# Conditioned ternary FFN on one Trainium2 core: the second block goes over from eight to seven products in its sixth chunk

## The chip, the cores and the metric

The kernel runs on one core of one Trainium2 chip. The core has five engines with a queue each: PE (TensorE, matmuls, with a separate weight load PEld), DVE (VectorE), ACT (ScalarE), POOL (GpSimd), and SP, which here only issues DMAs. Each queue runs its instructions in order; where one waits for another engine, all behind it wait too. The metric is the device time of one execution in microseconds, the median of three runs.

## The reference

`x` has the shape (128, 64, 512): 128 batch elements, 64 channels, 512 positions. Each batch element picks one of 200 weight matrices of 64 x 64, and its 64 x 512 slice is multiplied by it. The result goes through a feed-forward network whose two weight matrices are made ternary (each entry is -1, 0 or 1, times one scale alpha per matrix), and the output is rounded to 15 steps of one global scale and added to `x`:

```python
w = weights[conditions]
c = einsum('bct,bcd->bdt', x, w)                   # 128 x 64 x 512
h = gelu(c @ ternarize(W1).T + b1)                 # W1: 2048 x 512
y = h @ ternarize(W2).T + b2                       # W2: 512 x 2048
scale = max(abs(y)) / 7 + 1e-8
out = x + clip(round(y / scale), -7, 7) * scale
```

`ternarize` takes 0.05 of the largest absolute weight as its threshold; alpha is the mean absolute value of the weights above it. So alpha of W1 must be known before the first gelu, alpha of W2 before the first `y`.

## The kernel before

**Blocks and chunks.** The 8192 rows of the network (128 batch elements x 64) are worked in 16 blocks (`NB`) of 512 rows (`BLK`): eight batch elements each, as four pairs. The hidden width of 2048 is worked in 16 chunks (`NH`) of 128. For each block `n` and chunk `hc`, layer 1 multiplies the block's x (512 deep, four matmuls) by a chunk of W1 into PSUM, ACT takes the gelu, and layer 2 multiplies the result by the chunk's rows of W2 into four PSUM tiles `py0` to `py3`, which collect over all 16 chunks. Layer 2 of a chunk runs two steps after its layer 1 (`LAG = 2`).

**Two parts of everything.** Each operand is a sum of a high part in float32r and a low part in float16 (the remainder). Both are multiplied with the ternary weights. High products need the weights widened to float32r: POOL casts them (`widen1`, `widen2`, `widen7`). Low products take the narrow weights (float8, `w1t` and `w2t`) as they are. So layer 1 of a chunk is eight matmuls of 512 columns. ACT makes high parts (`split`, `up`), DVE makes low parts (`split`, `rest`, called by `low`).

**Eight products and seven.** From block 2 on, layer 1 is done for two chunks at a time by a scheme of Strassen's kind (`seven`): a two by two block product with seven half-size products in place of eight. It needs sums of the quarters of x (`condition7` makes them for the next block: `xb` the three quarters used as they are, `xt` the four sums, `xl` the low parts of all seven) and sums of the weights (`add_weights`, part 0 on POOL, part 1 on DVE, into `sums`). Its results are collected in the PSUM tiles `xy` and `z`, and put together by ACT copies and DVE adds into the buffers `ring`. Block 1 uses eight products in all its 16 steps (`eight`), and block 0 has a form of its own, while the weights are being made ternary.

**Order of the work.** The program's order is written out by hand: every engine call goes through `InOrder`, so the order of the Python calls is the order in each engine's queue. Pieces are placed behind matmuls by their step number: in `eight` by `hc`, in a pair by the calls `behind(0)` to `behind(6)` within `seven`.

**Around the change.** In the second half of block 0 (line 700 on) PE runs layer 2 of block 0. After its steps 5, 7, 9 and 11 one quarter of block 1's x is multiplied by its conditioned weights (`condition`, `mix`), ACT copies the high part, DVE subtracts for the low part, ACT counts the ternary entries of a quarter of W2 (`count2`) and casts that quarter to float8 (`kept(w2t, j, terns2)`), and DVE multiplies out the weights' sums (`sum2`). In block 1, step 1 finishes alpha of W2 (`alpha_2`) and the results of block 0 (`result`); step 2 takes the maxima of these results and stores them (`largest`, `keep`); steps 3 to 15 add up the weights for the seven products; steps 2 to 11 fetch, place and condition block 2's x; the last two steps widen the first weights for the seven products.

The pool `big` has 20 buffers of 8 KB a partition that are handed on from tile to tile; `ps_h` has two PSUM buffers, which layer 1's chunks take in turn, and later `xy`; `ps_c` has two, for the product of x with its weights, and later `z`.

Of the kernel before, what the change touches and what calls it, by code (L numbers as in the profile page):

```python
# [20 lines left out]
P = 128  # L21
# [18 lines left out]
def tile_cond_ternary_ffn(  # L40
# [26 lines left out]
    LAG = 2  # L67
    SEVEN = range(2, NB)
    HELD = NH // 2
# [3 lines left out]
    HALF = BLK // 2  # L73
    ADDED = [3, 4, 5, 6, 7, 12, 13, 14]

# [16 lines left out]
    def pair_of_pairs(h):  # L92
        return slice(h * PAIRS // 2, (h + 1) * PAIRS // 2)

    def load_x(n):

        xt = big.tile([P, PAIRS, T], F32, tag="big", name=f"xt_{n}")
# [92 lines left out]
    def parts(n):  # L190
# [268 lines left out]
    def layer2(n, hc, js=range(PAIRS), ks=(1, 0), ends=None):  # L459
        two = hidden[n, hc]  # L460
        w = wide2[n, hc], group2_of(hc) if n == 0 and hc < NH - LAG else w2t[:, hc]
# [238 lines left out]
    for hc in range(NH - LAG):  # L700
# [14 lines left out]
        if hc == 4:  # L715
            two_next = parts(1)
            w2t = big.tile([P, NH, T], F8, tag="big", name="w2t")
        if hc in (5, 7, 9, 11):
            j = (hc - 5) // 2
            condition(1, j, pair_of(x_next, j), two_next)  # L720
            count2(j)
            kept(w2t, j, terns2)
            if j == 0:
                signed2(3)
            if j == 1:
                for i in range(12, NH - 1):
                    low(0, i)
            for g in {9: [0, 1], 11: [2, 3]}.get(hc, []):
                sum2(g)
# [75 lines left out]
    def quarter_x(n, j):  # L805

        sp.dma_start(out=extra["x"][:, j % 2, :], in_=x_blk[n][:, j, :])

    def product(out, w, b, k, first=False, last=False):
        for c in range(2):  # L810
            pe.matmul(
                out=out,
                lhsT=w[k][:, c, :],
                rhs=b[k][:, c, :],
                start=(first and c == 0),
# [4 lines left out]
    def seven(n, k, behind, before, last):  # L820

        xb, xt, xl = cond[n]
        b11, b21, b22 = [(xb[:, i : i + 2], xl[:, i : i + 2]) for i in (0, 2, 4)]
        t1, t2, t3, t4 = [(xt[:, i : i + 2], xl[:, i + 6 : i + 8]) for i in (0, 2, 4, 6)]
        x, y = extra["xy"] if k % 2 == 0 else extra["xy"][::-1]
# [153 lines left out]
    def eight(s):  # L979

        n, hc = steps[s]
        if hc < NH - 1:
            widen1(n, hc + 1)
        else:
            widen7(0, 0)
        widen2(*steps[s + 1 - LAG])
        if hc == 0:
            extra["x"] = half.tile([P, 2, T], F32, tag="half", name="x_quarters")
            for j in range(2):
                quarter_x(n + 1, j)  # L990
# [17 lines left out]
        hidden[n, hc] = two  # L1008
        if hc == NH - 1:
            widen7(0, 1)  # L1010
        if 8 <= hc < 8 + PAIRS:
            j = hc - 8
            for part in condition7(n + 1, j, extra["x"][:, j % 2, :], two_next[-1]):
                part()
            if j + 2 < PAIRS:
                quarter_x(n + 1, j + 2)
            cond[n + 1] = two_next[-1]
        if hc == LAG:
            for j in range(PAIRS):
# [24 lines left out]
    def pair(n, k):  # L1044
# [10 lines left out]

        def behind(i):
            if i == 0 and n >= KNOWN:
                if n == KNOWN and k < 2:
# [186 lines left out]
```

## Time and profile before

| | |
|---|---|
| median of 3 runs | 963.0 us (962.86 to 963.06) |
| the profiled execution | 963.12 us |
| its span, from the first to the last instruction | 961.3 us |
| granted TensorE clock | 0.999 |
| PE busy | 949.9 us |
| POOL, DVE, ACT busy | 714.2, 710.6, 637.3 us |
| block 0, layer 2 begins | 51.49 us |
| block 1, layer 1 of its first chunk | 80.33 us |
| first pair with seven products (block 2) | 141.48 us |

Times in the traces are microseconds from the first instruction. A line of a timeline has start, duration, engine, kind, what it writes and reads with the shape, and in brackets how long the engine had been idle and which instruction released it. Buffer numbers are left out of names, so `x` stands for a tile of conditioned x, `ph` for a PSUM tile of layer 1, `py` for layer 2's. Consecutive matmuls overlap: a group's stated time is longer than the distance to the next one. As every call goes through one helper, all instructions show line 36 of the kernel; they are told apart by tile names.

### The profile page before, as it was taken

Reading aid. Unit: us, or ns where it says so; the run is one execution under the profiler, and the core shown is the slowest. Engines: PE = TensorE matmul, PEld = TensorE weight load, DVE = VectorE, ACT = ScalarE, POOL = GpSimd, SP = SyncE. Lnnn points to the kernel's source line nnn. Section 1 sums busy time; section 2 is a strip of 40 time slices with the busy share of each in tenths; the row PEclk is TensorE's granted clock in tenths of the full one; section 3 lists DMA queues with packets and bytes.
Section 4 is the critical chain, followed back from the end, with each engine's and each line's share of the span. In section 5 each row is a group of like instructions: output and inputs, shape, how many; then the busy total and the mean of one; then the engine's idle time right before and its main releaser. Section 6 shows DMA issues by size and latency. Waiting matters only on the chain.

```text
span 961.3 us, 17574 instructions
## 1 busy us (share of the span) xinstructions
PE 949.9 (99%) x6077; PEld 733.7 (76%) x6080; DVE 710.6 (74%) x1239; ACT 637.3 (66%) x1148; POOL 714.2 (74%) x1064
## 2 busy tenths in 40 slices
PE   8999999999999999999999999999999999999997
PEld 4666667888788787788778778788778878878784
DVE  7999766666676766666676676766667798888986
ACT  7995456656656566665666656666665777878784
POOL 5789867677686776767767686776768879788772
PEclk9999999999999999999999999999999999999999
DMA  9201011110111100111010111100131184575751
GB/s 357 105 23 47 14 33 49 32 62 15 35 48 35 60 24 25 52 41 49 25 70 14 35 50 33 59 26 24 49 121 60 49 304 170 180 248 169 276 203 62
DMA packets 33195, 80.11 MB, mean 83 GB/s; under 512 B 3792, under 2 KB 3792, under 8 KB 30160
## 3 DMA queue, kind: packets, MB, share of 16 engines
q1 hardware_dynamic: 31056, 76.86, 23.0%
q0 software_dynamic: 2048, 2.10, 0.7%
q8 instruction: 49, 0.80, 0.3%
q14 instruction: 42, 0.34, 0.1%
HBM read 46.44 MB, written 32.51 MB: 82 GB/s over the span
## 4 chain that ended last, share of the span: by engine, by line
PE 96%; DVE 2%; DMA 1%; ACT 0%; POOL 0%; issue 0%; SPq 0%; ACTq 0%
PE py L36 47%; PE xy L36 22%; PE z L36 16%; PE pc L36 6%; PE ph L36 6%; DVE top L36 1%; DMA nat<-in_L_ffn_W 1%; DVE xt L36 0%; DVE y_last L36 0%; ACT diag L36 0%; POOL wf L36 0%; PE number L36 0%; DVE terns L36 0%; DVE ymax L36 0%; DVE x L36 0%
## 5 line engine op out<-in xcount | busy, mean ns | idle before, releaser
L36 POOL CAST wf<-w2t 128x512 fp32r<-128x512 fp8e4 x240 | 228.8, 974 | 105.7 <-PE py L36 102.8
L36 PE MATMUL py<-wf,h 128*128 128x512 f32 x960 | 285.1, 418 | 0.0
L36 POOL CAST wf<-sums 128x256 fp32r<-128x256 fp8e4 (+1 forms) x336 | 182.6, 549 | 85.6 <-PE xy L36 81.9
L36 DVE SCALAR_TENSOR_TENSOR low_parts<-ring,h 128x512 f16<-128x512 f32 x228 | 203.0, 928 | 37.9 <-ACT h L36 37.7
L36 PE MATMUL py<-w2t,low_parts 128*128 128x512 fp8e4 x928 | 220.5, 379 | 0.0
L36 ACT ACTIVATE ring<-ring,b1t,alpha_up 128x512 f32<-128x512 f32 x216 | 175.2, 818 | 58.8 <-DVE ring L36 53.9
L36 DVE TENSOR_TENSOR ring<-xy,ring 128x256 f32<-128x256 f32 x216 | 119.8, 555 | 119.9 <-PE xy L36 118.4
L36 PEld LDWEIGHTS py<-wf,h 128*128 128x128 f32 x960 | 173.0, 189 | 39.1
L36 ACT COPY ring<-xy 128x256 f32<-128x256 f32 x216 | 80.6, 373 | 171.8 <-PE xy L36 171.2
L36 PEld LDWEIGHTS <-low_parts 128*128 128x128 f16 x928 | 90.4, 98 | 85.2 <-issue 0.3
L36 POOL CAST wf<-w1t 128x256 fp32r<-128x256 fp8e4 (+1 forms) x240 | 132.9, 570 | 2.8 <-POOL wf L36 0.4
L36 ACT ACTIVATE h<-ring 128x512 fp32r<-128x512 f32 x232 | 134.0, 627 | 0.6
L36 PE MATMUL xy<-xb,wf 128*128 128x256 f32 x448 | 98.8, 302 | 0.0
L36 PE MATMUL xy<-xt,wf 128*128 128x256 f32 x448 | 88.0, 277 | 0.0
L36 PE MATMUL xy<-xl,sums 128*128 128x256 f16 x448 | 87.9, 278 | 0.0
L36 PE MATMUL xy<-xl,w1t 128*128 128x256 f16 x448 | 86.8, 275 | 0.0
L36 PE MATMUL z<-xl,sums 128*128 128x256 f16 x448 | 85.5, 273 | 0.0
L36 PEld LDWEIGHTS xy<-xt,wf 128*128 128x128 f32 x448 | 76.3, 188 | 10.0
L36 PEld LDWEIGHTS xy<-xb,wf 128*128 128x128 f32 x448 | 75.9, 189 | 10.2
L36 PEld LDWEIGHTS <-sums 128*128 128x128 fp8e4 x896 | 69.2, 97 | 14.8
L36 POOL DMA_INDIRECT wg<-in_L_cond_weights,rows x64 | 64.2, 1003 | 18.3 <-issue 8.6
L36 PEld LDWEIGHTS <-w1t 128*128 128x128 fp8e4 x736 | 61.6, 98 | 18.1 <-issue 4.3
(139 smaller groups left out, 1410.0 us busy)
## 6 DMA issues: line engine op xcount, KB each, us to landing
xt<-in_x SPq DMA_DIRECT2D x36, 512.0 KB
y_dram<-y SPq DMA_DIRECT2D x15, 1024.0 KB
out<-xt SPq DMA_DIRECT2D x30, 512.0 KB
x_quarters<-in_x SPq DMA_DIRECT2D x56, 256.0 KB
nat<-in_L_ffn_W SPq DMA_DIRECT2D x6, 1024.0 KB
y_back<-y_dram SPq DMA_DIRECT2D x2, 1024.0 KB
nat<-in_L_ffn_W SPq DMA_DIRECT2D x3, 512.0 KB
wg<-in_L_cond_weights,rows POOLq DMA_INDIRECT x64, 2.5
```

Source lines behind the costliest of these rows:

```text
L36: return lambda *args, **kw: self._tc.keep_in_program_order(make(*args, **kw))
```

## The change

Block 1 uses eight products for its chunks 0 to 5 alone, and seven in five pairs for chunks 6 to 15 (`SWITCH = 3`: the first pair is number 3). For this:

- **The sums of block 1's x.** The quarters that the seven products need unsummed are read out of the existing `x0_1` and `x1_1` by strided views (`whole_parts`). For the sums, ACT keeps a float32 copy of the conditioned x: `condition(..., whole=True)` copies each PSUM tile once more, into the tile that x was loaded to. At the end of step 1 `sums_of_x` has DVE make the four sums in place (four instructions of 128x512) and ACT cast all of them to float32r (`xt_high`, 128x2048). In steps 3 and 4 `low_sums_of_x` makes their low parts (DVE, 128x1024 each).
- **W2 in float8.** The casts of quarters 2 and 3 (`kept(w2t, ...)`, ACT) move from block 0 into steps 0 and 1 of block 1. Layer 2 of block 0 takes narrow weights from `terns2` in all its chunks.
- **Sums of weights.** Numbers 3, 4 and 5 are made in steps 2 to 5, the rest within the pairs.
- **Maxima and store of block 0's results** move from step 2 to step 5. The first placement of block 2's conditioning weights moves from step 7 to step 5, the rest of block 2's conditioning into the pairs, as in other blocks. The gather of block 2's last quarter is issued in step 5 and once more in the first pair.

```diff
-    SEVEN = range(2, NB)
-    ADDED = [3, 4, 5, 6, 7, 12, 13, 14]
+    SWITCH = 3
...
+    def parts_of_1():
+        hi = big.tile([P, NT, BLK], F32R, tag="big", name="x0_1")
+        lows = big.tile([P, 2 * NT, BLK], F16, tag="big", name="x1_1")
+        high_sums = big.tile([P, PAIRS, T], F32R, tag="big", name="xt_high")
+        low_sums = lows[:, NT:, :].rearrange("p c t -> p (c t)")
+        return hi, lows[:, :NT, :], high_sums, low_sums.rearrange("p (j t) -> p j t", j=PAIRS)
...
-    def condition(n, j, xp, two):
+    def condition(n, j, xp, two, whole=False):
         pc = ps_c.tile([P, NT, P], F32, tag="pc", name=f"pc_{n}_{j}")
         mix(xp, j, pc)
         split(pc, *(t[:, :, j * P : (j + 1) * P] for t in two))
+        if whole:
+            act.copy(xp.rearrange("p (c t) -> p c t", c=NT), pc)
...
-            two_next = parts(1)
+            two_next = parts_of_1()
...
-            condition(1, j, pair_of(x_next, j), two_next)
+            condition(1, j, pair_of(x_next, j), two_next[:2], True)
             count2(j)
-            kept(w2t, j, terns2)
+            if j < 2:
+                kept(w2t, j, terns2)
...
+    def sums_of_x():
+        b11, b12, b21, b22 = (whole_sums(whole_x[1], r, h) for r in range(2) for h in range(2))
+        dve.tensor_tensor(b11, b12, b11, ALU.subtract)
+        dve.tensor_tensor(b12, b22, b12, ALU.subtract)
+        dve.tensor_tensor(b22, b22, b11, ALU.subtract)
+        dve.tensor_tensor(b21, b21, b22, ALU.subtract)
+        act.copy(cond[1][2], whole_x[1])
+
+    def low_sums_of_x(j):
+        js = pair_of_pairs(j)
+        dve.tensor_tensor(
+            cond[1][3][:, js], whole_x[1][:, js], cond[1][2][:, js], ALU.subtract
+        )
+
+    def whole_sums(t, r, h):
+        t = t.rearrange("p j (r c h d) -> p r c h j d", r=2, c=2, h=2)
+        return t[:, r, :, h]
+
+    def whole_parts(t, r, h):
+        t = t.rearrange("p (r c) (j h d) -> p r c h j d", r=2, h=2, d=C)
+        return t[:, r, :, h]
+
+    def operands(n):
+        if n == 1:
+            hi, lo, high_sums, low_sums = cond[n]
+            b = [(whole_parts(hi, *i), whole_parts(lo, *i)) for i in ((0, 0), (1, 0), (1, 1))]
+            t = [
+                (whole_sums(high_sums, *i), whole_sums(low_sums, *i))
+                for i in ((0, 0), (1, 1), (0, 1), (1, 0))
+            ]
...
     def eight(s):
         n, hc = steps[s]
-        if hc < NH - 1:
+        leaves = hc == 2 * SWITCH - 1
+        if not leaves:
             widen1(n, hc + 1)
         else:
-            widen7(0, 0)
+            widen7(SWITCH, 0)
         widen2(*steps[s + 1 - LAG])
...
+        if leaves:
+            place(n + 1, 0)
         if 2 <= hc < 2 + PAIRS:
             fetch(n + 1, hc - 2)
-        if 7 <= hc < 7 + PAIRS:
-            place(n + 1, hc - 7)
         for part in range(2):
-            if hc - part in ADDED:
-                add_weights(ADDED.index(hc - part), part)
-        if hc == NH - 2:
-            widen7(0, 2)
-            widen7(0, 3)
+            if 2 <= hc - part < 5:
+                add_weights(hc - part + 1, part)
+        if hc == 2 * SWITCH - 2:
+            widen7(SWITCH, 2)
+            widen7(SWITCH, 3)
+        if hc in (3, 4):
+            low_sums_of_x(hc - 3)
...
-        if hc == NH - 1:
-            widen7(0, 1)
-        if 8 <= hc < 8 + PAIRS:
...
+        if hc < 2:
+            kept(w2t, hc + 2, terns2)
+        if leaves:
+            widen7(SWITCH, 1)
-        if hc == LAG:
+        if hc == 2 * SWITCH - 1:
             for j in range(PAIRS):
                 largest(n - 1, j)
             keep(n - 1)
...
         low(n, hc)
+        if hc == 1:
+            sums_of_x()
...
         def behind(i):
+            if i == 0 and SWITCH < k + (n - 1) * NH // 2 <= NH // 2:
+                add_weights((k + 2) % (NH // 2), 1)
+            if i == 6 and n == 1:
+                add_weights((k + 3) % (NH // 2), 0)
...
-        if n in SEVEN:
-            if s == SEVEN[0] * NH:
+        if s >= NH + 2 * SWITCH:
+            if s == NH + 2 * SWITCH:
```

More of the change, by code (lines that the diff above doesn't have):

```diff
@@ L93, in pair_of_pairs @@
         return slice(h * PAIRS // 2, (h + 1) * PAIRS // 2)
+    whole_x = {}
     def load_x(n):
-        xt = big.tile([P, PAIRS, T], F32, tag="big", name=f"xt_{n}")
+        xt = whole_x[n] = big.tile([P, PAIRS, T], F32, tag="big", name=f"xt_{n}")
         for h in range(2):
@@ L460, in layer2 @@
         two = hidden[n, hc]
-        w = wide2[n, hc], group2_of(hc) if n == 0 and hc < NH - LAG else w2t[:, hc]
+        w = wide2[n, hc], group2_of(hc) if n == 0 else w2t[:, hc]
         begins, ends = ks[0], ks[-1] if ends is None else ends
@@ L807, in quarter_x @@
         sp.dma_start(out=extra["x"][:, j % 2, :], in_=x_blk[n][:, j, :])
+    def sums_of_x():
[24 more added lines that the diff above has]
+            ]
+        else:
+            xb, xt, xl = cond[n]
+            b = [(xb[:, i : i + 2], xl[:, i : i + 2]) for i in (0, 2, 4)]
+            t = [(xt[:, i : i + 2], xl[:, i + 6 : i + 8]) for i in (0, 2, 4, 6)]
+        return b + t
     def product(out, w, b, k, first=False, last=False):
@@ L813, in product @@
                 lhsT=w[k][:, c, :],
-                rhs=b[k][:, c, :],
+                rhs=b[k][:, c],
                 start=(first and c == 0),
@@ L820, in seven @@
     def seven(n, k, behind, before, last):
-        xb, xt, xl = cond[n]
-        b11, b21, b22 = [(xb[:, i : i + 2], xl[:, i : i + 2]) for i in (0, 2, 4)]
-        t1, t2, t3, t4 = [(xt[:, i : i + 2], xl[:, i + 6 : i + 8]) for i in (0, 2, 4, 6)]
+        b11, b21, b22, t1, t2, t3, t4 = operands(n)
         x, y = extra["xy"] if k % 2 == 0 else extra["xy"][::-1]
@@ L1008, in eight @@
         hidden[n, hc] = two
-        if hc == NH - 1:
-            widen7(0, 1)
-        if 8 <= hc < 8 + PAIRS:
[L1012 to L1017, printed above, removed]
-        if hc == LAG:
+        if hc < 2:
[3 more added lines that the diff above has]
+        if hc == 2 * SWITCH - 1:
             for j in range(PAIRS):
```

## The prediction

> **What bounds the kernel now.** I read four views of the profile in this order: the page's busy times and chain, the table of stretches across the end of the second block (block 1), the timelines of ScalarE (ACT), VectorE (DVE) and TensorE (PE) where block 0 hands over to block 1, and the groups of instructions by shape.
>
> ```profile
> PE 949.9 (99%) x6077; PEld 733.7 (76%) x6080; DVE 710.6 (74%) x1239; ACT 637.3 (66%) x1148; POOL 714.2 (74%) x1064
> ...
> PE 96%; DVE 2%; DMA 1%; ACT 0%; POOL 0%; issue 0%; SPq 0%; ACTq 0%
> ```
>
> PE is the bound: 949.9 of 961.3 us busy, 96% of the chain. Fewer products therefore show in the time, and so does every wait put in front of PE. The stretches below are two steps of eight products (127.14 and 134.32), three pairs of seven products without a product of x with its weights (148.28, 192.69, 199.50) and two pairs with one (161.89, 169.59).
>
> ```profile
> core 0: us, PE busy (x) PEld busy (x) DVE busy (x) ACT busy (x) POOL busy (x), PEclk, DMA share, GB/s
> 80.50:87.70 7.20, 7.20 (x35) 4.43 (x35) 6.96 (x11) 3.55 (x5) 7.17 (x5) 1.00 0.01 2
> ...
> 127.14:134.32 7.18, 7.18 (x34) 4.41 (x32) 5.15 (x11) 3.44 (x5) 6.12 (x8) 1.00 0.15 38
> 134.32:141.48 7.16, 7.16 (x34) 4.42 (x32) 4.58 (x7) 2.82 (x4) 5.85 (x9) 1.00 0.01 2
> ...
> 148.28:155.08 6.80, 6.80 (x45) 5.34 (x44) 6.47 (x11) 3.90 (x7) 5.28 (x9) 1.00 0.38 154
> ...
> 161.89:169.59 7.70, 7.70 (x54) 6.23 (x52) 4.57 (x12) 4.61 (x10) 6.61 (x12) 1.00 0.03 10
> 169.59:177.29 7.70, 7.70 (x54) 6.23 (x52) 5.26 (x13) 5.13 (x11) 5.67 (x10) 1.00 0.14 36
> ```
>
> PE has no idle time in any of them. But in the first stretch, where block 1 begins, DVE is busy 6.96 of 7.20 us and POOL (GpSimd) 7.17. That is where the change adds work, so I read it instruction by instruction. A line is start, duration, engine, what it writes and reads.
>
> ```profile
> 63.53 0.59 ACT L36 CAST x<-pc 128x512 fp32r<-128x512 f32 x1 [0.91 <-PE pc L36]
> 64.01 1.91 ACT L36 ACTIVATE masks<-terns 128x2048 bf16<-128x2048 bf16 x1
> 65.92 1.89 ACT L36 CAST w2t<-terns 128x2048 fp8e4<-128x2048 bf16 x1
> 68.00 0.59 ACT L36 CAST x<-pc 128x512 fp32r<-128x512 f32 x1 [0.20 <-PE pc L36]
> ...
> 72.48 0.59 ACT L36 CAST x<-pc 128x512 fp32r<-128x512 f32 x1 [0.20 <-PE pc L36]
> ```
>
> ```profile
> 65.15 0.68 DVE L36 TENSOR_TENSOR x<-pc,x 128x512 f16<-128x512 f32 x1
> ...
> 73.10 0.69 DVE L36 TENSOR_TENSOR x<-pc,x 128x512 f16<-128x512 f32 x1
> ...
> 79.20 0.68 DVE L36 TENSOR_TENSOR x<-pc,x 128x512 f16<-128x512 f32 x1
> ```
>
> ```profile
> 81.25 1.04 PE L36 MATMUL ph<-x,w1t 128*128 128x512 f16 x4
> ...
> 85.74 0.28 PE L36 MATMUL total<-sums,ones_f 128*128 128x8 f32 x2
> ...
> 94.87 1.08 PE L36 MATMUL ph<-x,wf 128*128 128x512 f32 x4
> ```
>
> ACT makes the high part of x for block 1 in four quarters (63.53, 68.00, 72.48, 76.95), DVE the low part (65.15, 69.87, 73.10, 79.20), and DVE does not idle once between 60 and 97 us. PE reads the last low part from 81.25, only 1.4 us after its end, and the sums for the second scale at 85.74, 0.7 us after DVE ends them (84.99).
>
> **The change part by part.**
>
> *Removed:* chunks 6 to 15 of block 1 become five pairs. Two steps take 7.17 us (mean of 7.18 and 7.16), a pair 6.80: 5 x 0.37 = 1.8 us saved on the path. A product of x with its weights costs the same in both forms (7.70 - 6.80 = 0.90 a pair, and 1.80 for the two in the 8.97 us from 109.20 to 118.17).
>
> *A, the float32 copy in block 0.* After each quarter's high part ACT copies the same PSUM tile once more (nearest row 0.59). In the built program this copy waits for DVE's low part of that quarter, and everything of ACT queues behind it. From the first quarter: low part ends 65.83; copy to 66.4; count (1.91) and cast to w2t (1.89) to 70.15, and only then the second high part, which stood at 68.00. Its low part ends 71.45, copy 72.05, count and cast 75.75, third high part to 76.35 (it began at 72.48). DVE, done with its three other instructions at 74.1, waits for it, and its third low part runs at 76.37 instead of 73.10: 3.27 late. The last two casts to w2t leave ACT here, but after this point. DVE's two sums of products (73.70 to 79.20, 5.5 us) follow, so the last low part ends at 83.15 where PE wants it at 81.25: stall 1.9. The other two (5.19 us) end at 88.3; the total, now due at 87.64, waits 0.7 more. **A = 2.6 us.**
>
> *B, the sums of x in chunk 1.* DVE is now 3.27 late, so its results of block 0 end at 93.3 instead of 90.06, just in time (PE's slack there was 0.7). Low part of chunk 1: 94.2. Then four sums of 128x512, each waiting for the one before. The trace has no such instruction. The nearest row, two SBUF operands of that size, is the low part of x_quarters: 0.69; the loaded rows of the low parts of h stand at 1.03 in the middle. I take 0.69 + 0.03 (nearest in kind); with 1.03 it is 1.4 more, and with 0.67 (the smallest row, a reduction) 0.1 less. They end at 97.1. ACT's copy of all of x to float32r (128x2048) waits for them: 1.89 by the casts of that size, 1.86 by the line through the 256 and 512 wide casts (0.38, 0.59). It ends at 99.0. Queued behind it on ACT stands the gelu of chunk 2, which was ready at 89.67; it ends at 99.8 and only then frees one of the two PSUM buffers that layer 1 of chunk 4 needs. That is due at 94.87 + 2.6 = 97.5. **B = 2.3 us.** The two casts to w2t moved here (3.8 us) lie between gelus, where ACT has 2.1 to 2.3 us free each time, and end at 92.3: nothing, as the copy is waiting for DVE anyway; if DVE were early they would show by up to 0.5.
>
> *C, POOL in chunk 5.* Its cast of the sums for the first pair waits for DVE's two weight sums (1.45), which stand behind the low part of chunk 2 (0.9), behind that gelu: 102.8. Then in POOL's queue: casts 0.61 + 0.40, w1t 0.94, w2t 0.73, the moved placement of weights 2 x 0.50, the moved gather DMA 0.99 (one of the four gathers of the next block is issued twice, 1 us of POOL more), and the two casts that the pair's second and third products read, 0.49 each: 107.9 and 108.3. PE is there at 107.2. **C = 1.0 us.**
>
> *D, DVE's backlog.* Behind the weight sums (102.8) stand two low sums of 128x1024 (1.25 each by the line through 0.415 for 256 and 0.690 for 512 wide; 2.1 if slowed like the low parts), two low parts (0.9 each), two more pairs of weight sums (1.45 each), the four maxima of block 0, moved here from chunk 2 (2.4), and the low part of chunk 5 (0.9): 113.1. ACT's copy of z (0.59) overwrites what that low part reads, and PE's third use of z waits for it: 113.7. PE, 2.3 us into its pair, is there at 110.3. **D = 3.4 us.** After that nothing is behind: DVE has 5.26 + 1.45 for its moved weight sums in a pair of 7.70, POOL 5.67 + 1.45. Only the first such pair (POOL 6.61 + 1.45) is over, by 0.4 at most, which I take as 0, since POOL idles in waits for PE there. SP issues the same DMAs; the store of y for block 0 goes out three chunks later, and nothing waits for it.
>
> *TensorE's reads.* In block 1 the pairs read x in runs of 64 values with gaps. No row has TensorE doing so. ACT moves 256 values in 4 runs of 64 in 0.373 us (copies of xy) and 0.378 (casts of pc): I take 0. The far end is the slowest matmul row, 0.111 us for 128 columns of plain float32 against 0.115 for 256 here: 140 such matmuls would cost 16 us more. Below nothing is excluded, as the columns stay the same.
>
> Sum: 2.6 + 2.3 + 1.0 + 3.4 - 1.8 = 7.5 us. The profiled execution took 963.12 us (span 961.3), 0.1 over the median of 963.0: **970.5 us**.
>
> [...]
>
> ```profile
> L36 DVE SCALAR_TENSOR_TENSOR low_parts<-ring,h x58: 680/1032/3667, 85.0 to 293.2; 128x512 f16<-128x512 f32 x58
> ```
>
> Low parts of h, with two SBUF inputs, scatter from 680 to 3667 ns, while x<-pc,x with one operand in PSUM stays at 0.68 to 0.69. [...]
>
> **The rivals.**
>
> 1. *The backlog never forms* (the other side). DVE's rows are stretched by something: 3.36 against 2.28 for the same sum of products, 1.77 against 0.68 for low parts. If the new order sets all of them beside an idle POOL, they run at their smallest. Then the last low part of x ends at 81.1, before 81.25: A = 0. B: 90.7 + 2.8 + 1.9 + 0.8 = 96.2 against 94.87, 1.3. C 0.2. D shrinks to 1.6 (DVE through at 106.9). 3.1 - 1.8 = +1.3: 964.4, within 0.2%. It decides at whether that last low part is done by 81.25. Against it: POOL is busy 2.8 of every 3 us from 60 to 96.
> 2. *All of it is hidden* and only the saving shows: 961.3. For it: PE idles nowhere now. Against: it needs the gelu of chunk 2 off the path too, and that waits for DVE in ACT's order.
> 3. *Heavier.* Low sums at 2.1 (+1.7), sums at 1.03 (+1.4), one low part of 3.67 in the backlog as at 101.92 (+2.8), or a part of the gap cost of TensorE's reads: 973.5 to 981.
>
> **How the numbers follow.** 0.2% is 1.9 us, about what a measurement of this kernel can tell from no change. Forecast (966 to 973.5): 0.70, all slower. Heavier: 0.16, slower. Backlog never forms (962.5 to 966): 0.09, of it 0.06 within, 0.02 slower, 0.01 faster. All hidden: 0.05, at the edge, 0.02 within, 0.03 faster. Slower 0.88, same 0.08, faster 0.04. The range of 965 to 975.5 leaves out most of the two lighter cases (0.13) and the upper half of the heavier one (0.07).
>
> **What would show it.** In the profile after: pairs from the sixth chunk at 6.8 us and 7.7 us; ACT's second copy of each quarter released by DVE; PE idle before the low half of layer 1 of chunk 0 (about 1.9 us), before layer 1 of chunk 4 released by ACT (2.3), and before z in the first pair (C and D). A last low part by 81.25 refutes A, a gelu of chunk 2 before 95 refutes B, no idle before z refutes C and D. A first pair that is long without PE idle would mean that the reads with gaps cost.

## The result: 0.9% slower, as forecast

| | before | after |
|---|---|---|
| median | 963.01 us (962.86 to 963.16, six runs) | 971.89 us (971.58 to 972.16, six runs) |
| profiled execution, its span | 963.12, 961.3 us | 972.08, 970.3 us |
| granted clock | 0.999 | 0.995 |

The ratio is 1.0092, with a 95% interval of 1.0079 to 1.0105. The forecast was 970.5 us in a range of 965.0 to 975.5, with 0.88 for slower. In all that follows, times in a trace are of one profiled execution; 165.59 us of before is an event that both traces have (the first product of x with its weights in block 2), and after reaches it 8.54 us later. Behind it the two run alike but for 0.4 us.

The busy times and the chain of after, from its page:

```profile
PE 952.9 (98%) x6140; PEld 740.0 (76%) x6140; DVE 720.6 (74%) x1260; ACT 646.0 (67%) x1168; POOL 723.8 (75%) x1080
...
PE 90%; DVE 6%; ACT 1%; DMA 1%; issue 1%; POOL 0%; SPq 0%; ACTq 0%; DVEq 0%
```

PE's share of the chain fell from 96% to 90% and DVE's rose from 2% to 6%: there are waits now. PE is busy 3 us longer although it has fewer columns to multiply, which no wait explains. The timelines of after say where. First ACT and DVE in block 0:

```profile
66.06 0.59 ACT L36 COPY xt<-pc 128x512 f32<-128x512 f32 x1 [1.74 <-DVE x L36]
...
75.75 0.59 ACT L36 CAST x<-pc 128x512 fp32r<-128x512 f32 x1
```

```profile
76.37 0.69 DVE L36 TENSOR_TENSOR x<-pc,x 128x512 f16<-128x512 f32 x1 [2.20 <-ACT x L36]
...
81.81 0.68 DVE L36 TENSOR_TENSOR x<-pc,x 128x512 f16<-128x512 f32 x1
```

The float32 copy is released by DVE's low part, and count, cast and the next high part stand behind it. The third low part starts at 76.37 in place of 73.10, the last at 81.81 in place of 79.20. Then PE, and ACT and DVE in the first steps of block 1:

```profile
82.54 1.02 PE L36 MATMUL ph<-x,w1t 128*128 128x512 f16 x4 [0.94 <-DVE x L36]
...
87.82 0.36 PE L36 MATMUL total<-sums,ones_f 128*128 128x8 f32 x2 [0.64 <-DVE sums L36]
...
102.34 2.05 PE L36 MATMUL ph<-x,wf 128*128 128x512 f32 x4 [5.16 <-ACT ring L36]
104.19 1.93 PE L36 MATMUL ph<-x,w1t 128*128 128x512 f16 x4
```

```profile
99.62 1.90 ACT L36 CAST xt_high<-xt 128x2048 fp32r<-128x2048 f32 x1 [8.36 <-DVE xt L36]
101.43 0.77 ACT L36 ACTIVATE ring<-ph,b1t,alpha_up 128x512 f32<-128x512 f32 x1
```

PE waits three times: for the last low part, for the sums of products, and then 5.16 us for the gelu of chunk 2 (101.43), which stands in ACT's queue behind the copy of the sums of x (99.62), which waits for DVE's four sums. And the matmuls after that wait take nearly twice as long as their like: 2.05 and 1.93 for four, where 1.08 and 1.04 are usual. The table of stretches has the reason in its column PEclk (behind POOL's):

```profile
core 0: us, PE busy (x) PEld busy (x) DVE busy (x) ACT busy (x) POOL busy (x), PEclk, DMA share, GB/s
...
97.20:102.30 5.10, 0.00 (x0) 0.00 (x0) 2.33 (x1) 2.58 (x3) 4.26 (x7) 0.85 0.05 13
102.30:108.55 6.25, 6.21 (x16) 3.34 (x17) 5.53 (x8) 3.33 (x5) 3.09 (x3) 0.57 0.01 3
108.55:112.13 3.58, 3.58 (x18) 2.21 (x16) 3.55 (x7) 1.41 (x2) 2.85 (x5) 1.00 0.00 0
112.13:120.17 8.04, 8.04 (x54) 6.35 (x53) 5.43 (x13) 4.61 (x10) 6.59 (x13) 1.00 0.04 10
120.17:127.87 7.70, 7.70 (x54) 6.25 (x53) 6.88 (x15) 5.13 (x11) 7.55 (x13) 1.00 0.13 34
143.30:150.10 6.80, 6.80 (x46) 5.35 (x45) 5.18 (x9) 4.52 (x8) 6.02 (x10) 1.00 0.03 9
```

While PE stood idle the granted clock fell to a half (0.50 from 100.8 to 107.6), and it stayed there for most of the step of chunk 4, which took 6.21 us where the next step takes 3.58. Then come the pairs: 8.04 us for the first, 7.70 for the second, 6.80 for the last in the table.

Counted from start to start against before, the 8.54 us at the common event are:

| | us |
|---|---|
| wait for the last low part of x | +1.09 |
| wait for the sums of products | +0.86 |
| wait for the gelu of chunk 2 | +5.31 |
| chunk 4 at half the clock (6.21 for 3.58, before rounding) | +2.62 |
| the remainder, the first pair being longer than the second (8.04 and 7.70) | +0.30 |
| five pairs for ten steps, by their usual lengths (7.70 or 6.80 a pair) | -1.84 |
| later start of the whole trace | +0.20 |

Why did four sums of 128x512, priced at 0.72 each, take 5.87 us? The durations of that group, then DVE's last one, then POOL beside it:

```profile
L36 DVE TENSOR_TENSOR xt<-xt x4: 693/1036/3003, 93.7 to 96.5; 128x512 f32<-128x512 f32 x4
```

```profile
96.53 3.00 DVE L36 TENSOR_TENSOR xt<-xt 128x512 f32<-128x512 f32 x1
```

```profile
96.64 1.24 POOL L36 TENSOR_TENSOR sums<-w1t 128x256 fp8e4<-128x256 fp8e4 x2
97.82 0.60 POOL L36 CAST wf<-w1t 128x512 fp32r<-128x512 fp8e4 x1
98.38 0.60 POOL L36 CAST wf<-w2t 128x512 fp32r<-128x512 fp8e4 x1
```

The first line gives smallest, median and largest: 0.69, 1.04, 3.00 for instructions of one shape. The longest stands beside a streak of POOL without a gap (96.64 to 98.98: two sums of weights, which like DVE's sums read two operands, and two casts) and ends 0.55 us behind it. Whether that is the cause is one of the questions below.

### The profile page after: what moved, and what is told of

It reads as the page before. It is cut to its first block, busy times and chain, and to the rows that moved or that the text cites. A ratio compares the mean times of both kernels' runs of the same rounds, so it can differ in the third digit from the quotient of the medians.

```text
span 970.3 us, 17754 instructions
## 1 busy us (share of the span) xinstructions
PE 952.9 (98%) x6140; PEld 740.0 (76%) x6140; DVE 720.6 (74%) x1260; ACT 646.0 (67%) x1168; POOL 723.8 (75%) x1080
## 4 chain that ended last, share of the span: by engine, by line
PE 90%; DVE 6%; ACT 1%; DMA 1%; issue 1%; POOL 0%; SPq 0%; ACTq 0%; DVEq 0%
PE py L36 43%; PE xy L36 22%; PE z L36 17%; PE pc L36 6%; PE ph L36 2%; DVE nat L36 1%; DVE low L36 1%; DVE xt L36 1%; DMA nat<-in_L_ffn_W 1%; DVE top L36 1%; DVE terns L36 1%; DVE junk L36 0%; ACT w2t L36 0%; DVE x L36 0%; DVE y_last L36 0%
## 5 line engine op out<-in xcount | busy, mean ns | idle before, releaser
L36 POOL CAST wf<-w2t 128x512 fp32r<-128x512 fp8e4 x240 | 232.4, 989 | 98.0 <-PE py L36 94.8
L36 POOL CAST wf<-sums 128x256 fp32r<-128x256 fp8e4 (+1 forms) x351 | 191.8, 552 | 91.1 <-PE xy L36 84.6
L36 ACT ACTIVATE ring<-ring,b1t,alpha_up 128x512 f32<-128x512 f32 x226 | 183.4, 818 | 60.5 <-DVE ring L36 55.2
L36 DVE TENSOR_TENSOR ring<-xy,ring 128x256 f32<-128x256 f32 x226 | 125.5, 555 | 120.6 <-PE xy L36 120.6
L36 ACT COPY ring<-xy 128x256 f32<-128x256 f32 x226 | 84.1, 372 | 181.8 <-PE xy L36 180.2
L36 POOL CAST wf<-w1t 128x256 fp32r<-128x256 fp8e4 (+1 forms) x240 | 129.5, 556 | 1.9
L36 PEld LDWEIGHTS <-sums 128*128 128x128 fp8e4 x936 | 72.4, 97 | 15.4
L36 POOL DMA_INDIRECT wg<-in_L_cond_weights,rows x65 | 66.5, 1023 | 18.8 <-issue 9.3
L36 DVE TENSOR_TENSOR ring<-z,ring 128x256 f32<-128x256 f32 x113 | 47.7, 422 | 41.0 <-PE z L36 40.4
```

The lines of the kernel that those rows point to most:

```text
L36: return lambda *args, **kw: self._tc.keep_in_program_order(make(*args, **kw))
```

## The experiments

Three questions were open after this. Are the waits separate costs, or do they stand in series behind each other, so that the longest hides the rest? Is the slow sum POOL's doing? And can the change be made without the waits, so that its 1.84 us show? Theory: DVE's, ACT's and POOL's queues each come late by a similar amount, so that PE waits for whichever is last. Rival: the copy on ACT (B in the prediction) is the cost, and without it the time falls by its wait. Each kernel below is the changed kernel with the edit shown.

**1. The copy of the sums behind gelu 2.**

```diff
 def sums_of_x():
...
-    act.copy(cond[1][2], whole_x[1])
 def eight(s):
...
     hidden[n, hc] = two
+    if hc == 2:
+        act.copy(cond[1][2], whole_x[1])
```

> Edit: ACT's copy of the sums of x to float32r is issued behind the gelu of chunk 2 instead of ahead of it. Theory (the gelu queued behind the copy starves TensorE for 5.3 us, and the halved clock after that idle time costs 2.6 us more): the idle time before layer 1 of chunk 4 and the slow matmuls go, the low part of chunk 2 behind VectorE's sums costs about 1.2 us, and up to 2.5 us of the waits before z come back: 965 to 968 us. Rival (VectorE's late sums are what counts, and TensorE only waits at its next need for the same time): 971 to 972 us.

Measured: 971.15 us (970.88 to 972.27), ratio 1.0088 (1.0071 to 1.0105). PE's waits in block 0 and block 1 (in total, times, longest):

```profile
PE z L36 <- POOL wf L36: 3.5, 1, 3.5
PE py L36 <- DVE low_parts L36: 1.5, 2, 1.2
...
```

The wait of 5.16 is gone, and the time is what it was. In its place PE waits 1.5 for low parts, which now stand behind the sums of x, and 3.5 in the first pair for POOL's casts; after that wait the clock is at a half for 3.4 us (109.9 to 113.3). The rival's 971 to 972 came, the theory's 965 to 968 did not. So it is the series, not the copy alone.

**2. TensorE kept at work.** 22 matmuls of 512 columns before layer 1 of chunk 4, into a PSUM tile that nothing reads.

```diff
 def eight(s):
...
+    if hc == 4:
+        idle = ps_c.tile([P, T], F32, tag="pc", name="idle_2")
+        for _ in range(22):
+            pe.matmul(out=idle, lhsT=cond[1][1][:, 0, :P], rhs=w1t[:, 0], start=True, stop=True)
     layer1(n, hc, ph)
```

> Edit: 22 matmuls of 512 columns into an unused PSUM tile, ahead of layer 1 of chunk 4, fill the 5.3 us in which TensorE is idle there; nothing reads them. Theory (the idle time lowers the granted clock to 0.5, and that alone makes the next 16 matmuls take 6.2 us instead of 3.6): layer 1 of chunk 4 starts at the same time, the clock stays at 1.0, and the time falls by 2.6 us to 969.3 us. Rival (those matmuls are slow because they wait for weights or operands): no gain, 971.9 us or a little more.

Measured: 973.06 us (971.81 to 973.19). The profiled execution is the one of 971.81:

```profile
102.03 1.16 PE L36 MATMUL ph<-x,wf 128*128 128x512 f32 x4 [0.42 <-ACT ring L36]
103.04 1.04 PE L36 MATMUL ph<-x,w1t 128*128 128x512 f16 x4
...
111.99 0.85 PE L36 MATMUL z<-xt_high,wf 128*128 128x256 f32 x4 [2.30 <-POOL wf L36]
```

The clock stayed at 1.00, and layer 1 of chunk 4 took its usual time: the slow matmuls of after come from the idle time in front of them. Of the 2.62 us regained, 2.30 are waited for POOL before the first z. So C of the prediction is there; in after it was covered by the slow clock. The forecast of 969.3 was missed for this reason; the rival's figure came, but its reason (weights or operands) is refuted by these rows. The three executions near 973.1 have no profile.

**3. The float32 copy behind count and cast** (A alone).

```diff
 def condition(n, j, xp, two):
...
-    if whole:
-        act.copy(xp.rearrange("p (c t) -> p c t", c=NT), pc)
+    return pc
...
             if j < 2:
                 kept(w2t, j, terns2)
+            act.copy(pair_of(x_next, j).rearrange("p (c t) -> p c t", c=NT), pc)
```

> Edit: in block 0 the float32 copy of each quarter of x is issued behind the count and the cast of that quarter, where VectorE's low part is already done. Theory (A and B are separate: the copy's wait for VectorE makes VectorE late by 3.3 us and TensorE by 1.9 us): the waits before the low half of chunk 0 and before the total go, ACT's third high part is back at about 73 us, and the time falls by 1.9 us to 970.0 us, if the sums of x then take the 6 us that they took. Rival (VectorE's sums wait for POOL in any case and end at the same time): the idle time before chunk 4 grows by what A loses, 971.9 us.

Measured: 969.83 us (969.70 to 970.28), 2.06 less than after. PE's waits:

```profile
PE ph L36 <- ACT ring L36: 5.1, 1, 5.1
PE z L36 <- POOL wf L36: 1.0, 1, 1.0
```

Both waits of block 0 are gone, and the time falls by about what they cost (1.95). What follows did not simply move up, though. The clock at a half, and the step of chunk 4:

```profile
99.94:103.35 3.41, 3.27 (x8) 1.76 (x9) 2.62 (x5) 1.93 (x3) 1.11 (x1) 0.50 0.00 0
100.08:105.30 5.22, 5.22 (x17) 3.00 (x18) 4.54 (x7) 3.28 (x5) 3.06 (x3) 0.69 0.00 0
```

After nearly the same wait (5.11 for 5.16) the clock was at a half for 3.41 us and not 6.83, and chunk 4 took 5.22 in place of 6.21; the 1.0 us so gained went into the wait for POOL's casts. A is a cost by itself, and it comes from the order on ACT, not from the copies' time.

**4. POOL's sums of weights away from the sums of x.** Those of number 4 go from step 3 to step 4.

```diff
-        for part in range(2):
-            if 2 <= hc - part < 5:
-                add_weights(hc - part + 1, part)
+        for part in range(2):
+            for k in {2: [3], 4: [4, 5]}.get(hc - part, []):
+                add_weights(k, part)
```

> Edit: POOL's weight sums number 4 move from step 3 to step 4, and VectorE's part of them from step 4 to step 5, so that no POOL tensor_tensor runs beside VectorE's last sum of x. Theory (that sum took 3.0 us instead of 0.7 because POOL ran two tensor_tensor and two casts back to back beside it): it falls to about 0.7, the idle time before chunk 4 from 5.3 to 3.0 us, which is shorter than the 3.6 us after which the clock fell, so that the clock stays up as well: 967.0 us (969.6 if the clock falls all the same). Rival (the sum is slow by itself, being in place and strided): 971.9 us.

Measured: 970.54 us (970.49 to 971.96), ratio 1.0078 (1.0061 to 1.0095). The group of the four sums, and PE's waits:

```profile
L36 DVE TENSOR_TENSOR xt<-xt x4: 692/1036/1274, 93.3 to 96.1; 128x512 f32<-128x512 f32 x4
```

```profile
PE ph L36 <- ACT ring L36: 3.4, 1, 3.4
PE z L36 <- POOL wf L36: 2.8, 1, 2.8
...
```

The longest sum took 1.27 in place of 3.00, the four 4.14 in place of 5.87, and the wait for the gelu shrank from 5.2 to 3.4; the clock stayed up there (1.00). The gain is waited for POOL again (2.8), so that the forecast of 967.0 was missed. The slow sum is POOL's doing, the total is not that sum's.

**5. POOL's casts for the first pair first.** `place` for block 2 behind them, and the gather of step 5, which the first pair issues once more, left out.

```diff
-        if leaves:
-            place(n + 1, 0)
-        if 2 <= hc < 2 + PAIRS:
+        if 2 <= hc < 1 + PAIRS:
             fetch(n + 1, hc - 2)
...
         if leaves:
             widen7(SWITCH, 1)
+            place(n + 1, 0)
```

> The first pair's casts on POOL stand ahead of the placing and gather of step 5 (place for block 2 goes behind them, and the gather of step 5, which the first pair issues once more anyway, is left out). Nothing else is changed. Theory, the two waits in series (the sums of x hold up gelu 2 and chunk 4 first, POOL's casts come second and are hidden by the first): in after the first pair waits for nothing of POOL, so 971.6 (971.0 to 972.0). Rival, POOL's queue is a cost beside the other: the casts come 2.5 us earlier and the time with them, 969.4.

Measured: 971.68 us (971.60 to 971.86). By itself POOL's order is worth 0.2, which is within the scatter of the executions, as the series has it: the wait for the gelu (5.2) comes first and covers POOL.

**6 and 7. Both edits, and the maxima.** Experiment 6 is the edits of 1 and 5 together. Experiment 7 moves block 0's maxima and store as well:

```diff
-        if hc == 2 * SWITCH - 1:
-            for j in range(PAIRS):
-                largest(n - 1, j)
-            keep(n - 1)
...
-                if k in (1, 2):
-                    for j in (2 * k - 2, 2 * k - 1):
+                at = k - 3 if n == 1 else k
+                if at in (1, 2):
+                    for j in (2 * at - 2, 2 * at - 1):
                         largest(n - 1, j)
...
-                if k == 2:
+                if k == (5 if n == 1 else 2):
                     keep(n - 1)
```

> The last two edits together: ACT's copy of the sums is issued behind gelu of chunk 2, and POOL's casts ahead of its placing and gather. Alone the one gave 971.15 and left TensorE waiting 3.45 for POOL's casts before the first z, after which the clock was halved for 3 us. If POOL's queue is the second limit and nothing else stands near it: 971.15 - 3.45 - 1.5 of the slow clock = 966.2. Rival: a third queue is as late, DVE's, where the four maxima of block 0 (2.46 us) stand ahead of the low part of chunk 5, and ACT's copy of z behind that; then the wait for POOL is gone and one for ACT or DVE stands within the first pair: 969 to 971.

> As the one before, and the four maxima of block 0 and its store moved from step 5 into pairs 4 and 5. By the rival there (DVE's maxima are the third limit) this is 2 to 3 us faster than the one before, 967.5 (966 to 968.5), and what is left is the 1.95 of the float32 copy, the 1.5 of the low parts behind the sums, and a wait of some 1 to 2 in the first pair. If the maxima held nobody up, it equals the one before.

Measured: 970.53 us (969.66 to 971.43) and 967.73 us (967.60 to 968.29). PE's waits in experiment 6:

```profile
PE z L36 <- ACT ring L36: 2.3, 1, 2.3
PE py L36 <- DVE low_parts L36: 1.5, 2, 1.2
PE z L36 <- POOL wf L36: 1.2, 2, 0.9
...
```

The 3.5 for POOL became 1.2, and a wait of 2.3 for ACT's copy of z came up in its place, the one that D of the prediction names (the copy overwrites what the low part of chunk 5 reads, and that stands behind the maxima). With the maxima moved it is gone, and the time is 2.8 lower by the medians, 1.9 by the two profiled executions (969.71 and 967.78). Experiment 6 thus came out as its rival said (969 to 971), and 7 as its forecast (966 to 968.5). There are three limits in a row: ACT's copy, POOL's casts, DVE's maxima.

**8. All queues at once.** The edits of 3, 5 and 7, and the sums of x behind the low part of chunk 2, their copy behind gelu 3, the low parts of the sums a step later.

```diff
+        if hc == 3:
+            act.copy(cond[1][2], whole_x[1])
...
-        if hc in (3, 4):
-            low_sums_of_x(hc - 3)
+        if hc in (4, 5):
+            low_sums_of_x(hc - 4)
...
-        if hc == 1:
+        if hc == 2:
             sums_of_x()
```

> All queues at once: the float32 copy behind count and cast, the sums of x behind the low part of chunk 2 instead of ahead of it, their copy on ACT behind gelu of chunk 3, the two low parts of the sums a step later, POOL's casts ahead of placing and gather, the maxima in pairs 4 and 5. If the nine microseconds are made of these waits and the clock that falls after the longest of them, nothing much is left of them and the 1.84 that the five pairs save begins to show: 963 (961.5 to 965). Rival: the work itself is too much for DVE or POOL in these six steps, and whatever is moved the delay appears elsewhere: 966 or more.

Measured: 967.31 us (966.53 to 968.64), ratio 1.0047 (1.0032 to 1.0062). The rival's figure. The four sums and PE's waits:

```profile
L36 DVE TENSOR_TENSOR xt<-xt x4: 691/891/3010, 92.3 to 97.2; 128x512 f32<-128x512 f32 x4
```

```profile
PE z L36 <- POOL wf L36: 1.8, 1, 1.8
PE z L36 <- DVE x L36: 0.7, 1, 0.7
...
```

Again one sum of 3.01, the third this time, beside another streak of POOL (94.27 to 96.60). And after waits of only 1.84 and 0.71 the clock was at a half from 107.1 to 110.5.

**9. POOL quiet beside the sums.** The edits of 8, and POOL's and DVE's sums of weights and the gathers in new places, of which the main lines are:

```diff
         if hc == 2:
+            add_weights(3, 0)
...
             widen7(SWITCH, 3)
+            add_weights(4, 0)
...
             place(n + 1, 0)
+            add_weights(5, 0)
+            fetch(n + 1, 1)
...
         if hc == 2:
+            add_weights(3, 1)
             sums_of_x()
```

> As the kernel with all queues moved (967.31, three waits of 1.84, 0.71 and 0.46 before the first pair's reads, and after them 3.5 us at half the clock), with POOL kept quiet beside the sums of x: its sums of weights for pairs 4 and 5 go behind the casts of step 4 and of step 5, DVE's parts of them into the first pair; DVE's part for the first pair stands ahead of the sums of x; the gathers for block 2 stand in steps 1 and 5 and in the first pair. Theory: one of the four sums took 3.0 us, in after as in the kernel with all queues moved, only because POOL worked through a streak beside it, and the waits before the first pair follow from that; without the streak the four take 2.8 to 3.5 us, no wait over 0.7 us is left, the clock stays up, and the time is 962.5 (961.3 to 964.0). Rival: the fourfold duration is the sums' own (their strided reads); then they take 5 us or more again, waits of 2 to 3 us remain, and it is 966 to 967.

Measured: 966.35 us (966.00 to 967.30), ratio 1.0036 (1.0024 to 1.0049). The four sums, PE's waits, and the sums over 13 stretches of 1 us from 99 to 112:

```profile
L36 DVE TENSOR_TENSOR xt<-xt x4: 685/836/980, 94.2 to 96.7; 128x512 f32<-128x512 f32 x4
```

```profile
PE xy L36 <- POOL wf L36: 0.9, 1, 0.9
PE z L36 <- POOL wf L36: 0.8, 1, 0.8
PE py L36 <- POOL wf L36: 0.8, 1, 0.8
...
```

```profile
sum 13.00, PE 12.09 PEld 8.88 DVE 10.03 ACT 7.78 POOL 12.32; mean PE 0.93 PEld 0.68 DVE 0.77 ACT 0.60 POOL 0.95
```

The time is the rival's, but its reason is refuted: without POOL's sums of weights beside them the four sums took 3.44 us, 0.69 to 0.98 each, so their strided reads are not what made one take 3 us. POOL did not rest there, it cast:

```profile
95.15 0.93 POOL L36 CAST wf<-w2t 128x512 fp32r<-128x512 fp8e4 x1 [1.61 <-PE py L36]
96.02 1.87 POOL L36 CAST wf<-sums 128x512 fp32r<-128x512 fp8e4 x2
```

So this streak of casts alone made no sum take more than 0.98. The clock stayed up too (1.00 in each of the 13 stretches). What the expectation had missed is that POOL itself is now full, 12.32 of 13 us, and the three waits are for its casts.

**10 to 12. POOL's and DVE's work spread.** In 10, POOL's sums of weights for pair 4 go to step 3, those for pair 5 and later one pair on, and a gather into each of the first two pairs. In 11 those for pair 4 go one step on, to step 4, and one maximum stands in each of pairs 4 to 7. In 12 those for pair 4 go behind the first pair's casts, and both low parts of the sums stand in step 4. The core of 12 against 9:

```diff
-            add_weights(4, 0)
-        if hc in (4, 5):
-            low_sums_of_x(hc - 4)
+        if hc == 4:
+            low_sums_of_x(0)
+            low_sums_of_x(1)
...
             widen7(SWITCH, 1)
+            add_weights(4, 0)
             place(n + 1, 0)
-            add_weights(5, 0)
             fetch(n + 1, 1)
...
+            made = {3: [5], 4: [6], 5: [7], 6: [0], 7: [1, 2]}
+            if i in (0, 4):
+                for m in made.get(at - 1, [])[i // 4 : i // 4 + 1]:
+                    add_weights(m, 1)
+            if i == 6:
+                for m in made.get(at, []):
+                    add_weights(m, 0)
```

> As the quiet kernel (966.35; the four sums took 3.44 us there, the clock stayed up, and TensorE waited 0.83, 0.90 and 0.76 for POOL's casts in the first two pairs, where POOL was busy 12.3 of 13 us), with POOL's work spread: its sums of weights for pair 4 go into the gap of 1.6 us that it had in step 3, those for pair 5 to the end of the first pair, one set a pair from there, and the last two gathers into the first two pairs, one each. Theory: what is left of the loss is the amount of POOL's work in these steps; with 1.7 us of it taken from ahead of the first pair's casts and another 2.3 from the first pair the three waits go, and it is 964.0 (962.5 to 965.5). Rival: POOL stays full (its casts are stretched beside DVE's operations with two inputs), and waits of 2 us or more for it stay: 966 or more.

> As the spread kernel (964.60). There a low part took 3.47 us beside POOL's streak and held TensorE up for 0.63, the last low part of the sums for 0.35, and in pairs 5, 6 and 7 three waits for ACT's copy of z (0.19, 0.45, 0.21, some 1.0 with what goes with them) came of DVE being full (12.5 of 13 us) with two maxima a pair. Edit: POOL's sums of weights for pair 4 one step later, in the gap after its cast; one maximum a pair in pairs 4 to 7; the second set of DVE's sums of weights from pair 6 to the first pair of block 2. Theory: these waits are all that is left beside a later tail of 0.5, and the change then shows its saving: 963.0 (962.0 to 963.8), within 0.2% of before. Rival: DVE or POOL stay full and the waits only move: 964.3 or more.

> As the even kernel (964.25, 962.94 to 964.71). There the only long wait left was 1.21 before the first pair's product with the second half of x's low sums; ahead of that DVE's first sum of weights took 2.59 us and the sums of x 3.93 beside POOL's streak, which the sums of weights for pair 4 had made longer. Edit: these go behind the casts for the first pair, and DVE makes both low parts of the sums one after the other, ahead of the low part of chunk 4. Theory: the low parts end 2 us earlier (1 from the order, 1 from POOL's shorter streak), the wait goes, and the time is 963.0 (962.0 to 963.8): within 0.2% of before, at best 0.1% faster. Rival: a wait of 1 us or more for POOL's casts takes its place, 964.3 or more.

| | median (lowest to highest) | ratio, 95% |
|---|---|---|
| 10 | 964.60 (964.49 to 964.82) | 1.0017 (1.0007 to 1.0026) |
| 11 | 964.25 (962.94 to 964.71) | 1.0011 (1.0002 to 1.0020) |
| 12 | 963.66 (963.43 to 964.19) | 1.0009 (1.0000 to 1.0018) |

In 10, which kept its forecast (964.0, 962.5 to 965.5), no wait for POOL is left; those that remain are of DVE and of what ACT waits for:

```profile
PE z L36 <- ACT ring L36: 0.9, 3, 0.5
PE py L36 <- DVE low_parts L36: 0.6, 1, 0.6
PE z L36 <- DVE x L36: 0.4, 1, 0.4
```

The 0.6 is again a low part slowed to 3.47 us beside POOL's longer streak in step 3. Experiment 11 did not keep its forecast (962.0 to 963.8): its placing of the same sums lengthened the streak beside DVE's sums once more (one of DVE's sums of weights took 2.59 there, 1.38 in experiment 9), and the waits moved into one for DVE. What the profiles of 11 and 12 have left:

```profile
PE z L36 <- DVE x L36: 1.2, 1, 1.2
PE z L36 <- ACT ring L36: 0.2, 1, 0.2
```

```profile
PE z L36 <- ACT ring L36: 0.5, 1, 0.5
```

Experiment 12 kept its forecast (962.0 to 963.8). So 8.2 of the 8.9 us came back with the change's arithmetic untouched, by order, and with one gather of POOL less (the one that the change issues twice; a gather took 0.96 to 1.25 us of its queue in after). Nearly all of the loss is an affair of the order. No kernel here beat the one before: 12 lies 0.7 us above it, at the edge of its interval. At the common event it is 0.36 behind (the start of the trace set aside), so 2.2 us still cover the 1.84 saved: the wait of 0.5, and pairs that are longer with no wait listed in them (8.11 and 8.10 for the second and third, in place of 7.70). In its stretch from 111 to 124 POOL is busy 12.60 of 13 us, in before 7.33; that the rest is POOL's and DVE's amount of work, which no order removes, is argued from this and not shown.

## Why the prediction was right, and where it was not

The sign, the median (970.5 against 971.9) and the places of the waits were right. The sizes were not, and errors of opposite signs cancelled.

| step of the prediction | predicted | measured |
|---|---|---|
| removed: five pairs | -1.8 | -1.84 |
| A, float32 copy in block 0 | 2.6 | 1.95 (experiment 3: 2.06) |
| B, sums of x in front of gelu 2 | 2.3 | 5.31 |
| clock after B | not named | 2.62 |
| C and D, POOL's casts and DVE's backlog | 4.4 | 0.30 |
| TensorE's reads with gaps | 0 | 0 |
| later start, tail | 0 | 0.6 |

- **Removed.** Pairs of 7.70 and 6.80 us, as read from block 2.
- **A.** The mechanism held: third low part foreseen at 76.37, measured 76.37 in a trace that starts 0.20 later. The size was off since one of DVE's two sums of products, taken at the 3.36 it had had, took 2.69; both together fell from the 5.5 us of the prediction to 4.83 (76.98 to 81.81). Experiment 3 shows that the cause is what stands behind the copy.
- **B.** The chain held (sums, copy, gelu 2, PSUM buffer, chunk 4), and the copy took 1.90 where 1.89 was said. The mis-sized term is the four sums: 2.9 us said, 5.87 measured. The prediction took 0.72, after the row nearest in kind (the low part of x_quarters, 0.69), where the low parts of h, which it showed, scatter from 0.68 to 3.67, and kept a low part of 3.67 for rival 3 alone. Experiments 4 and 9 show that POOL's sums of weights beside them make the difference: 5.87 us for the four with them, 4.14 and 3.44 without.
- **The clock** was in no step. Every wait was priced at its own length, and the wait of 5.16 cost 2.62 more, that of 5.11 in experiment 3 still 1.64 (5.22 for 3.58). Experiment 2 shows it: with TensorE kept at work the matmuls took their usual time.
- **C and D.** By the prediction's own sign (no idle before z) both fell. They were priced on top of B as it was said, with PE at the first z at 107.2; PE came there at 112.50, and by then POOL and DVE had nearly caught up. DVE's low part of chunk 5 was to end at 113.1 and ended at 113.89, which is near by luck: the backlog began at 102.96 where 100.45 follows from the prediction, and took 10.93 in place of 12.65. (Two sums of the prediction are slightly off: the terms of C lead to 108.45 where it says 108.3, those of D to 113.3 where it says 113.1.) Experiments 1, 2, 4 and 6 bring both out again as soon as B shrinks: 2.3 to 3.5 for POOL, 2.3 for ACT behind the maxima. So the mechanisms were right, and adding them was right only for the B assumed: the true sum of the series is set by the latest queue.
- **TensorE's reads.** The pairs in block 1 of after take as long as those of block 2 in before (7.70 and 6.80 us). The choice of 0 between far ends was right.
- **Two operands in SBUF.** x<-pc,x, with one operand in PSUM, kept its 0.68 and 0.69 in before and after; the four sums, with both in SBUF, took 0.69 to 3.00 in after. In size the 1.03 each that the prediction names beside its 0.72 was also too low (4.1 us for the four, measured 5.87), as it is a median of durations with a long tail; that the 1.4 more which it gives for this makes 971.9 in all, as measured, is luck. How POOL holds such an operation up is not shown by any run here; what the rows show is one that lasts through several POOL instructions (3.00 us beside two sums of weights and two casts).
- **Rivals.** Rival 1 (backlog never forms) decided at a last low part by 81.25; it ended at 82.49. Rival 2 (all hidden) needed the gelu of chunk 2 off the path; it is what PE waited 5.16 us for. Rival 3 (heavier) named a slow operation of the kind that came (a low part of 3.67; it was one of the sums, 3.00), and the time is between the forecast and its 973.5.

## What to carry to other kernels

When several in-order queues are late by similar amounts, their waits are not a sum: the latest covers the others, and removing it alone returns little (here 0.7 of 5.2 us), so before pricing such a series walk all queues once with each term at its far end. A two-input DVE operation next to a streak of POOL work with two-input operations in it should be priced by the largest duration of its kind and not by the usual one (here 3.00 to 3.67 us for 128x512, where the median of the low parts of h in before is 1.03), and a long wait in front of TensorE at more than its length (2.6 and 1.6 us more for waits of 5.16 and 5.11). A change that saves on the bounding engine by adding work to others pays only as far as their queues have gaps where that work must stand, which is read from the stage and not from the page's shares (74% for each of DVE and POOL in before, and POOL 10.66 of 11 us from 99.5 to 110.5, where the new work was put).

## What the runs showed of the hardware that was not expected

- **The clock stood at a half for 3.4 us, once for 6.8.** From tables of 1 us stretches: in after PE is idle from 97.2 to 102.3, and the granted clock is at 0.50 from 100.8 to 107.6, 6.8 us. In experiments 1, 3, 4 and 8 it is at 0.50 for 3.4 us (109.9 to 113.3, 99.9 to 103.4, 112.0 to 115.4, 107.1 to 110.5), after waits of 3.45, of 5.11, of 2.85, and of 1.84 and 0.71 close together. It begins 3.3 to 5.0 us after the idle time does, in experiments 4 and 8 when PE is already back at work. Waits of 5.16 and 5.11 thus brought 6.8 us of it and 3.4. A wait of 3.44 in experiment 4 and one of 2.30 in experiment 2 did not lower it. The stretch of after in which it falls and the one in which it comes back:

```profile
100.20:101.20 1.00, 0.00 (x0) 0.00 (x0) 0.00 (x0) 1.00 (x1) 0.98 (x3) 0.80 0.06 16
...
107.30:108.30 1.00, 1.00 (x5) 0.81 (x4) 1.00 (x2) 0.30 (x1) 0.30 (x1) 0.84 0.00 0
```

  With 0.80 and 0.84 as means of 1.00 and 0.50, it fell at 100.2 + 0.6 and rose at 107.3 + 0.3. The length of an idle time alone does not decide whether it falls: in experiments 4 and 8 no idle time where the clock fell is longer than 2.85 us, and after the 3.44 of experiment 4 it was at 1.00 up to 112.0. What decides it no run here shows.
- **Executions of one kernel then differ by more than 1 us.** Experiments 2, 4 and 6 have two groups of times each (971.81 and 973.1; 970.5 and 971.96; 969.7 and 971.4). The profiled execution of experiment 4 belongs to its longer group and has 3.4 us at half the clock; those of 2 and 6 belong to the shorter and have none after their waits of 2.30 and 2.3. That the same wait lowers the clock in one execution and not in another would explain it; with one profile of each kernel this is argued and not shown. The mean clock of each execution does not settle it: the longer ones have the lower clock in experiments 2 and 6 (0.997 for 0.999, 0.996 and 0.997 for 0.998), but not in 4 (0.996, the others 0.995 and 0.996), and half a clock behind the last matmul, 1.7 to 5.0 us of the span in the profiles (2.6 in before, 2.5 in after), moves this mean as well.
- **A DVE operation with two operands in SBUF lasted through several POOL instructions.** 3.00, 3.01 and 3.47 us in place of 0.69 in after and in experiments 8 and 10, and POOL's cast of 0.60 us took up to 1.61 beside DVE's two-input operations in experiment 9. In each trace, all such operations of 128x512 that took 3 us or more (the low part of 3.67 in before too) stand beside a streak with two or four of POOL's sums of weights in it; beside casts alone, over 200 of them in a trace, the longest took 1.14 in before, 1.10 in after and 1.70 in experiment 11. Not every streak with sums does it (0.72 to 1.49 beside two of them elsewhere), and why is open.
